# A two-layer recurrent block: the second attention's division moved to DMA and GpSimd, and q, k kept in DRAM with 32 rows to a head

## The chip, the cores and the metric

The kernel runs on one core of one Trainium2 chip. The metric is the device time of one execution in microseconds (us): the median over several runs. Engines are named as in the profile: PE is TensorE (PEld its weight loads), DVE is VectorE, ACT is ScalarE, POOL is GpSimd, and SP is SyncE, which here only issues DMA transfers. Each engine works through its own instructions in a fixed order; an instruction that waits holds up all that stand behind it on that engine. That holds for SP too, so a transfer that waits for its source delays the transfers behind it.

## The reference

Two layers follow each other on x of 2 x 2048 tokens with 256 features. Each layer normalizes x, computes an attention s and a gate g = silu(ffn), and adds s * g to x. All is float32. The attention has 16 heads of 16 features; the first layer's sees all tokens, the second's only a band of 64 tokens to either side.

```python
def attention(x, w_qkv, b_qkv, w_out, b_out):        # second layer; the first has no mask
    q, k, v = split_heads(x @ w_qkv + b_qkv)         # (b, 16 heads, 2048, 16)
    scores = einsum('bhqd,bhkd->bhqk', q, k) * SCALE + mask
    attn = softmax(scores, axis=-1)
    out = einsum('bhqk,bhkd->bhqd', attn, v)
    return merge_heads(out) @ w_out + b_out
x = L0_attn_x
for attn, ffn in ((L0_attn, L0_ffn), (L1_attn, L1_ffn)):
    xn = layernorm(x)
    x = x + attn(xn) * silu(ffn(xn))
```

The first layer's ffn is a mixture of eight low-rank experts with a cumulative sum over tokens, the second's a base product with eight small experts. The change does not touch their arithmetic.

## The kernel before

x, the normalized xn and the gates gt lie in SBUF with the features in the partitions: 128 partitions, two halves of features (NC = 2), 2048 tokens, one tile for each of the two batches b. The stages follow each other: layer norm and products of weights, the first ffn (`hidden`, `weights`, the loop over `ch` with `we`, `px`, `py`, `po`), `attention(A0, ..., False, False)`, the second layer norm with its ffn, and `attention(A1, ..., True, True)`. In the last call `local` is true: the band.

`attention` works on items (b, g, n): batch, group g of four heads (NG = 4), block n of 512 tokens (TB); 32 items a layer, n innermost. Q and K are projected by `keys_queries`, given their bias by ACT and stored to the DRAM tile qd; `fetch` brings a group's q and k back, so that each of the four heads has 32 partitions (HP = 32) of which 16 (HD) hold features. Four small matmuls then run side by side on PE. In k the 17th row of a head is 1, and in q it holds minus the row's maximum, so that the product gives scores less the maximum. The other rows of q are zero: a zero row set comes from the DRAM tile zd. Two q and two k tiles take turns, so a group is fetched while the one before it is worked on; in the second layer in two halves of 1024 tokens.

An item takes U steps: 16 in the first layer, 2 in the second. A step of `scores` issues PE's products sq (queries in the partitions, for the maxima) of an item some steps ahead, and sk (keys in the partitions) of the current one. DVE reduces sq to maxima (L611, in the second layer L606 with the mask), ACT takes the exponentials of sk (L615), and in the second layer POOL clears what lies outside the band (`affine_select`, L620). `place_max` (L631 on) turns an item's maxima by a PE transpose pmx, DVE negates them (row, L638), and four DMAs put them into q. This stands LEAD = 3 steps before the item's first sk. `weigh` multiplies the exponentials with v, DEL steps later (acc, L662). v has a column of ones per head, so acc holds in rows HD of each head's 32 the sum by which the head must be divided; ACT (and in the first layer POOL, L673) gathers acc in av. In PSUM, the tag "m" of pool `pm` has four banks, shared by sk, acc, pmx, tr, of and pr; pool `pmax` has two for sq.

The division differs in the two layers. In the first, `compact` sends the sums of av to DRAM (rd) and the 16 data rows of each head straight to xn; `invert` fetches the sums as 128 x 16 (dn) and takes the reciprocal on DVE; `spread` writes them to DRAM and fetches them broadcast to 16 rows per head (recb); `divide` multiplies on POOL (L753). In the second, `normalize` transposes av by four PE transposes (tr, L687), DVE takes reciprocals (L689) and multiplies (L690), and when the four groups of a block are done, `features` transposes back (of, L703) and ACT copies (L705). `project` then multiplies with the output weights (pr, L761), DVE with the gate (upd, L766), POOL adds to x (L767), and in the last layer the block is sent out (L769).

When a part runs is given in steps: the loop calls `at(step, f, ...)`, and after each step's products the parts due are issued. The build then orders the instructions of each engine by these and by what they depend on; `tc.keep_in_program_order` holds an instruction at the place where it was written.

```python
at(i * U - LEAD, place_max, i)
end = (i + 1) * U
if local:
    at(end + DEL, normalize, i)
```

Of the kernel before, what the change touches and what calls it, by code (L numbers as in the profile page):

```python
# [10 lines left out]
F32 = mybir.dt.float32  # L11
# [6 lines left out]
P = 128  # L18
D = 256
# [18 lines left out]
def two_layers(ctx: ExitStack, tc: tile.TileContext, a, out):  # L38
# [113 lines left out]


    with tc.tile_pool(name="fw", bufs=1) as fw:
        FV = fw.tile([P, NC, 2 * KE * R0], F32, name="FV")
# [246 lines left out]
    def attention(A, scale, local, final):  # L402
# [14 lines left out]
        with ExitStack() as st:  # L417
            pool = lambda name, bufs, **kw: st.enter_context(tc.tile_pool(name=name, bufs=bufs, **kw))
            kq, vp, dr = pool("kq", 1), pool("vp", 1), pool("dr", 1, space=bass.MemoryType.DRAM)
            qd = dr.tile([2, B, D, T], F32, name="qd")  # L420
            vs = [vp.tile([P, NV, (H - 1) * HV + HP], F32, name=f"v{b}", tag=f"v{b}") for b in range(B)]
            qs = [kq.tile([P, T], F32, name=f"q{i}", tag=f"q{i}") for i in range(2)]
            ks = [kq.tile([P, T + 2 * PAD], F32, name=f"k{i}", tag=f"k{i}") for i in range(2)]
            zd = dr.tile([NG, T], F32, name="zd")

            rd = [[dr.tile([NG, TB], F32, name=f"rd{i}{k}", tag=f"rd{i}{k}") for k in range(2)] for i in range(2)]
            for t in qs:
                nc.gpsimd.memset(t, 0.0)
# [80 lines left out]
            def fetch(bg, lo=0, hi=T):  # L509

                if bg >= B * NG:
                    return
                b, g = divmod(bg, NG)
                k0, k1 = max(lo - PAD, 0), (T if hi == T else hi - PAD)
                for i, t in ((1, qs[bg % 2]), (0, ks[bg % 2])):
                    to, s = (slice(lo, hi), slice(lo, hi)) if i else (slice(PAD + k0, PAD + k1), slice(k0, k1))
                    for j in range(NG):
                        h = g * NG + j
                        nc.sync.dma_start(out=t[j * HP : j * HP + HD, to], in_=qd[i, b, h * HD : (h + 1) * HD, s])

                nc.sync.dma_start(out=qs[bg % 2][HD:P:HP, lo:hi], in_=zd[:, lo:hi])

# [107 lines left out]
            def place_max(i):  # L630
# [43 lines left out]

            def heads(b, n):

                return xn[0 if local else b].rearrange("p c t -> p (c t)")[:, bass.ts(n, TT * D)].rearrange(
                    "p (t h w) -> p t h w", h=H, w=HD
                )

            def normalize(i):

                b, g, n = items[i]
                av = avs.pop(i)
                ps = pm.tile([P, TT, NG, HP], F32, name="tr", tag="m")
                for t in range(TT):
                    nc.tensor.transpose(ps[:, t].rearrange("p j w -> p (j w)"), av[:, bass.ts(t, P)], ident)  # L687
                rec = op.tile([P, TT, NG], F32, name="rec", tag="rec", bufs=2)
                nc.vector.reciprocal(rec, ps[:, :, :, HD])  # L689
                nc.vector.tensor_tensor(  # L690
                    heads(b, n)[:, :, g * NG : (g + 1) * NG, :], ps[:, :, :, :HD],
                    rec[:, :, :, None].to_broadcast([P, TT, NG, HD]), ALU.mult,
                )

            feats = {}

            def features(i, c):

                b, g, n = items[i]
                ot = heads(b, n).rearrange("p t h w -> p t (h w)")  # L700
                ps = pm.tile([P, TB], F32, name="of", tag="m")
                for t in range(TT):
                    nc.tensor.transpose(ps[:, bass.ts(t, P)], ot[:, t, bass.ts(c, P)], ident)  # L703
                f = op.tile([P, TB], F32, name="f", tag=f"f{c}", bufs=2 if local else 1)
                nc.scalar.copy(f, ps)  # L705
                feats[b, n, c] = f

            def together(b, g, n):


                lo = g % 2 * NG * HD
                return xn[b][lo : lo + NG * HD, g // 2, bass.ts(n, TB)]

            divs = {}

            def compact(i):

                b, g, n = items[i]
                av = avs.pop(i)
                nc.sync.dma_start(out=rd[i % 2][0], in_=av[HD:P:HP, :])  # L720
                for j in range(NG):
                    nc.sync.dma_start(out=together(b, g, n)[j * HD : (j + 1) * HD, :], in_=av[j * HP : j * HP + HD, :])

            def flat(d):
                return d.rearrange("j (r e) -> (j r) e", r=P // NG)

            def invert(i, step):

                if step == 0:
                    divs[i] = op.tile([P, NG * TB // P], F32, name="dn", tag="dn", bufs=2)  # L730
                    tc.keep_in_program_order(nc.sync.dma_start(out=divs[i], in_=flat(rd[i % 2][0])))
                else:
                    tc.keep_in_program_order(nc.vector.reciprocal(divs[i], divs[i]))

            def spread(i, step):

                b, g, n = items[i]
                if step == 0:
                    tc.keep_in_program_order(nc.sync.dma_start(out=flat(rd[i % 2][1]), in_=divs[i]))
                    return  # L740
                recb = op.tile([P, TB], F32, name="recb", tag="recb", bufs=2)
                lo = g % 2 * NG * HD
                for j in range(NG):
                    tc.keep_in_program_order(nc.sync.dma_start(
                        out=recb[lo + j * HD : lo + (j + 1) * HD, :], in_=rd[i % 2][1][j, :].partition_broadcast(HD)
                    ))
                divs[i] = recb[lo : lo + NG * HD, :]

            def divide(i):

                b, g, n = items[i]
                tc.keep_in_program_order(
                    nc.gpsimd.tensor_tensor(together(b, g, n), together(b, g, n), divs.pop(i), ALU.mult)  # L753
                )

            def project(i, oc):
# [3 lines left out]
                for c in range(NC):  # L760
                    nc.tensor.matmul(  # L761
                        pr, A["o"][:, c, bass.ts(oc, P)], feats[b, n, c] if local else xn[b][:, c, cols],
                        start=(c == 0), stop=(c == NC - 1),
                    )
# [16 lines left out]
            for i, (b, g, n) in enumerate(items):  # L781
                at(i * U - LEAD, place_max, i)
                end = (i + 1) * U
                if local:
                    at(end + DEL, normalize, i)
                    if g == NG - 1:
                        for c in range(NC):
                            at(end + DEL + 1 + c, features, i, c)
                        for oc in range(NC):
                            at(end + DEL + 3 + oc, project, i, oc)  # L790
                else:

                    for r, (f, *step) in enumerate(
                        ((compact,), (invert, 0), (invert, 1), (spread, 0), (spread, 1), (divide,))
                    ):
                        at(end + DEL + (0, 2, 4, 5, 7, 11)[r], f, i, *step)
                    if g == NG - 1:
                        for oc in range(NC):
                            at(end + DEL + 13 + oc, project, i, oc)
                if local and n == NB // 2 - 1:  # L800
# [218 lines left out]
```

## Time and profile before

| what | value |
|---|---|
| median of 3 runs | 2620.93 us (2620.79 to 2621.52) |
| profiled execution, its own time | 2619.84 us |
| its span, first to last instruction | 2618.1 us |
| mean granted TensorE clock | 0.991 |
| PE busy | 2570.3 us (98% of the span) |
| DVE, ACT, POOL busy | 1671.5, 1641.1, 894.9 us |
| first layer's attention in the span | about 475 to 2142 us |
| second layer's attention | about 2246 to 2618 us |

The profile shows one execution. Busy times are shares of an engine's own span; since matmuls are pipelined and their ends are modelled, a busy PE is read for where it stands idle rather than as a measure of its rate. A group of instructions is given with its source line, engine, tile names, shape, count, busy time, mean duration, and the idle time before it with what ended it. The timeline gives starts and durations; a bracket holds the idle time before an instruction and what ended it. SPq is the issuing of transfers on SP.

### The profile page before, as it was taken

To read this page: it belongs to the slowest core of one execution; us is meant where nothing else is said; L and a number is where in the kernel's file an instruction comes from. 1 tells how busy PE (TensorE), PEld (TensorE's weight loads), DVE (VectorE), ACT (ScalarE), POOL (GpSimd) and SP (SyncE) were. 2 spreads that over 40 slices of the span, in tenths; PEclk is the share of its full clock that TensorE was granted. 3 is DMA by queue.
4 is the path that set the end of the run, shared out by engine and by line. 5 is a ranking of instruction groups with operands and counts; after the bars stand their busy time and mean duration, and the time that the engine had idled before them with its cause. 6 is when DMAs were issued, how large, how long until landed. Compare 5 with 4: busy or idle time off the path is not lost.

```text
span 2618.1 us, 49275 instructions
## 1 busy us (share of the span) xinstructions
PE 2570.3 (98%) x19060; PEld 1099.6 (42%) x19060; DVE 1671.5 (64%) x2753; ACT 1641.1 (63%) x3200; POOL 894.9 (34%) x845
## 2 busy tenths in 40 slices
PE   8999999999999999999999999999999978999999
PEld 5444444543333333333333333333333324558776
DVE  4133332167888888888777888888888523228884
ACT  5300000228888888888778888888888854236655
POOL 0000000203444444444444444444444430206666
PEclk9999999999999999999999999999999989989999
DMA  4031110410001010010010010010000012411120
GB/s 150 3 88 45 53 45 32 99 64 4 8 12 19 8 24 9 6 25 8 6 25 8 6 25 8 6 27 6 8 8 6 10 30 35 96 67 39 46 58 35
DMA packets 58857, 82.08 MB, mean 31 GB/s; under 512 B 24160, under 2 KB 29152, under 8 KB 57040
## 3 DMA queue, kind: packets, MB, share of 16 engines
q1 hardware_dynamic: 56576, 77.36, 12.3%
q8 instruction: 150, 2.46, 0.4%
q10 hardware_dynamic: 2048, 1.58, 0.2%
q14 instruction: 83, 0.68, 0.1%
HBM read 52.22 MB, written 21.95 MB: 28 GB/s over the span
## 4 chain that ended last, share of the span: by engine, by line
PE 97%; DVE 1%; ACT 1%; DMA 0%; issue 0%; POOL 0%; SPq 0%; POOLq 0%; ACTq 0%; DVEq 0%
PE sk L599 25%; PE acc L662 22%; PE sq L599 19%; PE pp L446 4%; PE py L377 4%; PE po L357 4%; PE px L373 4%; PE ph L263 2%; PE pr L761 2%; PE pp L459 2%; PE psf L199 1%; PE po L909 1%; PE tr L687 1%; PE xb L127 1%; PE po L389 1%; PE xt L104 1%
## 5 line engine op out<-in xcount | busy, mean ns | idle before, releaser
L611 DVE TENSOR_REDUCE part<-sq 128x2 f32<-128x1024 f32 x1024 | 1206.7, 1220 | 304.2 <-PE sq L599 303.7
L615 ACT ACTIVATE e<-sk 128x512 f32<-128x512 f32 x2048 | 1062.7, 615 | 214.9 <-PE sq L599 192.2
L599 PE MATMUL sk<-q,k 32*128 32x512 f32 (+2 forms) x5632 | 1149.7, 533 | 0.6 <-ACT e L615 0.4
L599 PE MATMUL sq<-k,q 32*128 32x512 f32 (+2 forms) x5120 | 1140.8, 572 | 3.2 <-DVE part L611 1.7
L673 POOL TENSOR_TENSOR av<-av,more 128x512 f32<-128x512 f32 x480 | 607.7, 1266 | 961.2 <-ACT more L672 961.1
L599 PEld LDWEIGHTS sk<-q,k 32*128 32x128 f32 x5632 | 532.3, 184 | 581.1 <-ACT e L615 490.9
L662 PE MATMUL acc<-e,v 128*32 128x512 f32 x4096 | 550.6, 605 | 0.0
L599 PEld LDWEIGHTS sq<-k,q 32*128 32x128 f32 x5120 | 412.5, 184 | 28.0 <-DVE part L611 14.0
L672 ACT COPY more<-acc 128x512 f32<-128x512 f32 x480 | 287.8, 600 | 3.8 <-PE acc L662 1.7
L662 PEld LDWEIGHTS acc<-e,v 128*32 128x32 f32 x4096 | 82.4, 108 | 391.5 <-ACT e L615 387.0
L393 ACT ACTIVATE gt<-po 128x512 f32<-128x512 f32 x16 | 9.5, 596 | 324.6 <-PE po L389 324.6
L606 DVE CUSTOM_DVE_ANT_0 seen<-sq,mask 128x256 f32<-128x256 f32 (+1 forms) x512 | 177.4, 411 | 41.5 <-PE sq L599 32.8
L399 POOL TENSOR_TENSOR x<-x,up 128x512 f32<-128x512 f32 x16 | 20.2, 1264 | 416.4 <-DVE up L396 416.4
L620 POOL TENSOR_SCALAR_AFFINE_SELECT xn<-xn 128x512 f32<-128x512 f32 x172 | 103.1, 635 | 119.3 <-ACT xn L615 117.4
L381 DVE TENSOR_TENSOR xs<-we,px 128x512 f32<-128x512 f32 x64 | 43.8, 685 | 135.4 <-PE px L373 135.4
L373 PE MATMUL px<-xn,FV 128*128 128x512 f32 x256 | 121.2, 595 | 0.0
L377 PE MATMUL py<-cum,FW 128*128 128x512 f32 x256 | 120.5, 593 | 0.6 <-DVE cum L346 0.6
L615 ACT ACTIVATE xn<-sk 128x512 f32<-128x512 f32 x172 | 90.1, 601 | 48.2 <-PE sk L599 12.9
L357 PE MATMUL po<-pr,UO 128*128 128x512 f32 x256 | 119.0, 592 | 0.0
L383 DVE TENSOR_TENSOR pr<-xs,py 128x512 f32<-128x512 f32 x64 | 44.0, 687 | 62.4 <-PE py L377 62.2
L766 DVE TENSOR_TENSOR upd<-gt,pr 128x512 f32<-128x512 f32 x32 | 22.0, 687 | 86.0 <-PE pr L761 79.5
L357 PEld LDWEIGHTS po<-pr,UO 128*128 128x128 f32 x256 | 48.6, 190 | 61.2 <-issue 60.7
(169 smaller groups left out, 1683.2 us busy)
## 6 DMA issues: line engine op xcount, KB each, us to landing
we<-wd SPq DMA_DIRECT2D x128, 128.0 KB
qd<-sb SPq DMA_DIRECT2D x48, 256.0 KB
k<-qd SPq DMA_DIRECT2D x40, 128.0 KB
q<-qd SPq DMA_DIRECT2D x40, 128.0 KB
x<-in_x SPq DMA_DIRECT2D x8, 512.0 KB
q<-row SPq DMA_DIRECT2D x256, 2.0 KB
xn<-av SPq DMA_DIRECT2D x128, 32.0 KB
recb<-rd SPq DMA_DIRECT2D x128, 32.0 KB
```

Of the source, the lines that this page charges most:

```text
L357: nc.tensor.matmul(po[oc], UO[:, ch, bass.ts(oc, P)], pr, start=(ch == 0), stop=False)
L373: nc.tensor.matmul(px, FV[:, c, bass.ts(ch, P)], xn[b][:, c, cols], start=(c == 0), stop=(c == NC - 1))
L377: nc.tensor.matmul(py, FW[:, c, bass.ts(ch, P)], cum[:, c, :], start=(c == 0), stop=(c == NC - 1))
L446: nc.tensor.matmul(ps, w[:, c, bass.ts(hf, P)], xn[b][:, c, bass.ts(n, TB)], start=(c == 0), stop=(c == NC - 1))
L599: nc.tensor.matmul(o, lhs, rhs, start=True, stop=True)
L606: nc.vector.tensor_tensor_reduce(seen[:, lo:hi], sq[:, d, t * 2 * P + lo : t * 2 * P + hi], mask[:, lo:hi], 1.0, LOWEST, ALU.add, ALU.max, ...
L611: nc.vector.tensor_reduce(pt[:, pair[0] : pair[1] + 1, t, kb], sq, AX.X, ALU.max)
L615: nc.scalar.activation(e, t, AF.Exp, scale=scale)
L620: nc.gpsimd.affine_select(out=e[:, :, c, :], in_=e[:, :, c, :], compare_op=ALU.is_ge, fill=0.0, base=0, pattern=[[0, 4], [sign, P]], chann ...
L662: nc.tensor.matmul(acc[hp[j], o : o + hi - lo], vs[b][:, kt, vcols(g, j)], es[j][:, lo:hi], start=(r == 0), stop=(r == len(parts) - 1), sk ...
L672: nc.scalar.copy(more, acc)
L673: nc.gpsimd.tensor_tensor(avs[i], avs[i], more, ALU.add)
```

## The change

qd becomes one DRAM tile for both layers with 32 rows to a head, of which the 16 rows that are not features are filled once, early in the first ffn's stage: with ones for k, zeros for q. A group's q or k is then one transfer of 128 rows, and zd and the settings of q and k by POOL are left out. `place_max` writes an item's maxima by one transfer.

The division goes the same way in both layers: `away` sends av whole to DRAM (ad), `compact` fetches the sums (dn) and the data rows (to xn) in one transfer each, `invert` takes the reciprocal on DVE and writes it to DRAM, `spread` fetches it broadcast in one transfer, and `divide` multiplies on POOL. These steps stand 0, 1, 2, 3 and 5 steps after an item's last `weigh` in the second layer, and the projection 6 after it. `normalize` and `features` are gone.

```diff
+    qd = ctx.enter_context(tc.tile_pool(name="qd", bufs=1, space=bass.MemoryType.DRAM)).tile(
+        [2, B, H, HP, T], F32, name="qd"
+    )
...
+        zeros = fw.tile([P, TB], F32, name="zeros")
+        nc.vector.memset(zeros, 0.0)
+        for b in range(B):
+            for i, t in ((0, ones), (1, zeros)):
+                for half in range(NC):
+                    nc.sync.dma_start(
+                        out=qd[i, b, bass.ts(half, H // NC), HD:, :], in_=t[:, None, :].to_broadcast([P, NB, TB])
+                    )
...
-            qd = dr.tile([2, B, D, T], F32, name="qd")
-            zd = dr.tile([NG, T], F32, name="zd")
-            rd = [[dr.tile([NG, TB], F32, name=f"rd{i}{k}", tag=f"rd{i}{k}") for k in range(2)] for i in range(2)]
-            for t in qs:
-                nc.gpsimd.memset(t, 0.0)
-            for t in vs + ks:
+            ad = [dr.tile([NG, HP, TB], F32, name=f"ad{i}", tag=f"ad{i}") for i in range(3)]
+            rd = [dr.tile([NG, TB], F32, name=f"rd{i}", tag=f"rd{i}") for i in range(3)]
+            for t in vs:
                 nc.gpsimd.memset(t, 1.0)
-            nc.sync.dma_start(out=zd, in_=qs[0][:NG, :])
...
-                nc.sync.dma_start(out=qd[i, b, bass.ts(hf, P), bass.ts(n, TB)], in_=sb)
+                nc.sync.dma_start(out=qd[i, b, bass.ts(hf, H // NC), :HD, bass.ts(n, TB)], in_=sb)
...
-                    for j in range(NG):
-                        h = g * NG + j
-                        nc.sync.dma_start(out=t[j * HP : j * HP + HD, to], in_=qd[i, b, h * HD : (h + 1) * HD, s])
-                nc.sync.dma_start(out=qs[bg % 2][HD:P:HP, lo:hi], in_=zd[:, lo:hi])
+                    nc.sync.dma_start(out=t[:, to], in_=qd[i, b, bass.ts(g, NG), :, s].rearrange("h w t -> (h w) t"))
...
-                for j in range(NG):
-                    nc.sync.dma_start(
-                        out=q[j * HP + HD : j * HP + HD + 1, bass.ts(n, TB)].rearrange("o (t c) -> o t c", c=P),
-                        in_=row[j * TT : (j + 1) * TT, :],
-                    )
+                nc.sync.dma_start(out=q[HD:P:HP, bass.ts(n, TB)].rearrange("j (t c) -> j t c", c=P), in_=row)
...
-                    avs[i] = op.tile([P, TB], F32, name="av", tag="av", bufs=2)
+                    avs[i] = op.tile([P, TB], F32, name="av", tag="av", bufs=3 if local else 2)
...
+            pin = tc.keep_in_program_order
+            def away(i):
+                pin(nc.sync.dma_start(out=ad[i % 3].rearrange("j w f -> (j w) f"), in_=avs.pop(i)))
...
+            def compact(i):
+                divs[i] = op.tile([P, NG * TB // P], F32, name="dn", tag="dn", bufs=3)
+                pin(nc.sync.dma_start(out=divs[i], in_=ad[i % 3][:, HD, :].rearrange("j (r e) -> j r e", r=P // NG)))
+                pin(nc.sync.dma_start(out=together(*items[i]), in_=ad[i % 3][:, :HD, :]))
+            def invert(i):
+                pin(nc.vector.reciprocal(divs[i], divs[i]))
+                pin(nc.sync.dma_start(out=flat(rd[i % 3]), in_=divs[i]))
+            def spread(i):
+                lo = items[i][1] % 2 * NG * HD
+                recb = op.tile([P, TB], F32, name="recb", tag="recb", bufs=2)
+                divs[i] = recb[lo : lo + NG * HD, :]
+                pin(nc.sync.dma_start(out=divs[i], in_=rd[i % 3][:, None, :].to_broadcast([NG, HD, TB])))
...
-                        pr, A["o"][:, c, bass.ts(oc, P)], feats[b, n, c] if local else xn[b][:, c, cols],
+                        pr, A["o"][:, c, bass.ts(oc, P)], xn[0 if local else b][:, c, cols],
...
+                hops = (0, 1, 2, 3, 5, 6) if local else (0, 2, 4, 7, 11, 13)
+                for hop, f in zip(hops, (away, compact, invert, spread, divide)):
+                    at(end + DEL + hop, f, i)
+                if g == NG - 1:
+                    for oc in range(NC):
+                        at(end + DEL + hops[-1] + oc, project, i, oc)
```

More of the change, by code (lines that the diff above doesn't have):

```diff
@@ L673, in weigh @@
                     nc.gpsimd.tensor_tensor(avs[i], avs[i], more, ALU.add)
[L675 to L706, printed above, removed]
@@ L708, in together @@
             def together(b, g, n):
                 lo = g % 2 * NG * HD
-                return xn[b][lo : lo + NG * HD, g // 2, bass.ts(n, TB)]
+                return xn[0 if local else b][lo : lo + NG * HD, g // 2, bass.ts(n, TB)]
             divs = {}
[L716 to L722, printed above, removed]
+            pin = tc.keep_in_program_order
@@ L724, in flat @@
+            def away(i):
+                pin(nc.sync.dma_start(out=ad[i % 3].rearrange("j w f -> (j w) f"), in_=avs.pop(i)))
             def flat(d):
                 return d.rearrange("j (r e) -> (j r) e", r=P // NG)
[L727 to L740, printed above, removed]
-                recb = op.tile([P, TB], F32, name="recb", tag="recb", bufs=2)
[L742 to L746, printed above, removed]
+            def compact(i):
+                divs[i] = op.tile([P, NG * TB // P], F32, name="dn", tag="dn", bufs=3)
+                pin(nc.sync.dma_start(out=divs[i], in_=ad[i % 3][:, HD, :].rearrange("j (r e) -> j r e", r=P // NG)))
+                pin(nc.sync.dma_start(out=together(*items[i]), in_=ad[i % 3][:, :HD, :]))
@@ L751, in divide @@
                 b, g, n = items[i]
-                tc.keep_in_program_order(
+                pin(
                     nc.gpsimd.tensor_tensor(together(b, g, n), together(b, g, n), divs.pop(i), ALU.mult)
@@ L783, in attention @@
                 end = (i + 1) * U
[L784 to L799, printed above, removed]
+                hops = (0, 1, 2, 3, 5, 6) if local else (0, 2, 4, 7, 11, 13)
[4 more added lines that the diff above has]
+                        at(end + DEL + hops[-1] + oc, project, i, oc)
                 if local and n == NB // 2 - 1:
```

## The prediction

> **What bounds the kernel now.** I read the page first, for the chain that ended last: it is TensorE almost throughout.
>
> ```profile
> PE 97%; DVE 1%; ACT 1%; DMA 0%; issue 0%; POOL 0%; SPq 0%; POOLq 0%; ACTq 0%; DVEq 0%
> ```
>
> So an edit is worth what it takes off PE's queue, and costs whatever makes PE wait. The stretches are next (length, busy time and count by engine, clock, DMA share, GB/s): the second layer's attention, and the end of the span.
>
> ```profile
> 2400.00:2500.00 100.00, 99.48 (x1641) 77.01 (x1635) 80.46 (x424) 61.36 (x128) 64.47 (x102) 1.00 0.18 52
> 2590.00:2618.00 28.00, 22.11 (x159) 12.02 (x158) 7.09 (x13) 7.00 (x14) 13.71 (x15) 0.97 0.20 75
> ```
>
> PE is full in the loop, but DVE (80%) and POOL (64%) are not far off. The groups by shape give what goes (tr, of) and what POOL does and will do more of:
>
> ```profile
> L687 PE MATMUL tr<-ident,av 128*128 128x128 f32 x128 | 20.5, 283 | 0.0
> L703 PE MATMUL of<-ident,xn 128*128 128x128 f32 x64 | 9.8, 276 | 0.0
> L620 POOL TENSOR_SCALAR_AFFINE_SELECT xn<-xn 128x512 f32<-128x512 f32 x172 | 103.1, 635 | 119.3 <-ACT xn L615 117.4 <-PE acc L662 1.1 <-PE sq L599 0.8
> L753 POOL TENSOR_TENSOR xn<-xn,recb 64x512 f32<-64x512 f32 x32 | 40.6, 1269 | 11.2 <-DMA recb<-rd 10.0
> ```
>
> Their means overlap in the pipeline, so the timeline of one item (two steps) gives the price:
>
> ```profile
> 2560.30 0.35 PEld L599 LDWEIGHTS sk<-q,k 32*128 32x128 f32 x3
> ...
> 2563.02 2.40 POOL L620 TENSOR_SCALAR_AFFINE_SELECT xn<-xn 128x512 f32<-128x512 f32 x4 [1.23 <-ACT xn L615]
> ...
> 2563.55 0.42 PEld L687 LDWEIGHTS tr<-ident,av 128*128 128x128 f32 x4 [0.20 <-ACT xn L615]
> ...
> 2564.14 0.19 PEld L599 LDWEIGHTS sk<-q,k 32*128 32x128 f32 x2 [0.17 <-ACT av L667]
> ...
> 2567.58 0.35 PEld L599 LDWEIGHTS sk<-q,k 32*128 32x128 f32 x3
> ```
>
> The step with the four transposes takes 3.84 us (2560.30 to 2564.14), the next, with a pmx in their place, 3.44: an item is 7.28. The first layer already divides by DMA, and its last item shows the chain bare:
>
> ```profile
> 2125.23 0.53 SPq L720 DMA_DIRECT2D rd<-av  x1
> ...
> 2128.32 0.53 SPq L731 DMA_DIRECT2D dn<-rd  x1
> 2130.04 0.25 DVE L733 RECIPROCAL dn<-dn 128x16 f32<-128x16 f32 x1 [7.56 <-DMA dn<-rd]
> 2130.32 0.34 SPq L739 DMA_DIRECT2D rd<-dn  x1
> 2131.76 1.71 SPq L744 DMA_DIRECT2D recb<-rd  x4
> 2135.18 1.26 POOL L753 TENSOR_TENSOR xn<-xn,recb 64x512 f32<-64x512 f32 x1 [9.98 <-DMA recb<-rd]
> ```
>
> A read of sums lands 1.72 us after its issue, a write of inverses 1.44, the spread 3.42.
>
> **The change part by part.**
>
> 1. Transposes gone. For the 28 items whose normalize stands before the last steps: the four transposes fill 0.43 us of PE (0.107 apart), and PE then waits 0.17 for av's copy because tr holds one of four PSUM banks. Between 0.43 and 0.60 an item; I take 0.55, near the upper end, since the bank is freed too: 28 x 0.55 = 15.4. For batch 0's last group `features` goes as well: 8 x 0.43 = 3.4. Together -18.8. On DVE the 0.25 + 0.42 us of L689 and L690 become one 0.24 reciprocal (L733's row); ACT loses sixteen 0.60 us copies. Both lie beside PE and count nothing.
>
> 2. POOL. Each item adds one 1.27 us multiply to eight selects of 0.60 (four in 2.40 above): 6.1 us of an item that PE would do in 6.7. It fits, barely. The multiply stands between the selects in POOL's order; a step's selects are then done some 6.4 us into the step and PE's acc reads them at about 8.9 (two steps later), so 1.27 more is covered by 2.5 us. Were that cover gone, an item would cost POOL's time.
>
> 3. The DMA hops, per item: away (256 KB), dn, xn, rd, recb, where there was none. In SP's order, per item: row, rd(i), away(i+1), recb(i), dn(i+1), xn(i+1). The reciprocal is fixed in DVE's order and the multiply in POOL's. Behind a late reciprocal stand the next eight maxima of DVE, then PE, with two sq buffers only. The loop: after recip(i), rd issues (0.4 us), then away(i+1), landing 2.1 (1.44 for a write, plus 256 KB at the rate below, 0.7), dn 2.0, reciprocal 0.25: 4.8 us, against 6.7 an item. 1.9 us are spare. recb lands some 4 us before POOL's multiply. [...]
>
> ```profile
> 2270.00:2271.00 1.00, 1.00 (x4) 0.48 (x3) 0.00 (x0) 0.41 (x1) 0.00 (x0) 1.00 0.61 229
> 2284.00:2285.00 1.00, 1.00 (x6) 0.87 (x6) 0.56 (x2) 0.00 (x0) 0.00 (x0) 1.00 1.01 123
> ```
>
> The first row (2 KB stores of q, k) is 229 / 0.61 = 375 GB/s, 23 an engine. On 4 engines recb's 128 KB take 1.4 us, so it lands in 2.9; on 16 it would be 1.8. [...]
>
> 4. Fetches. A group's q, k go from 1 MB in 16-row pieces (plus zeros) to 2 MB in 128-row transfers. The second row above is the old form at full load: 123 GB/s. [...] At 123 GB/s a half fetch of both would hold the rings 8 us; at 375, 2.8. I take 2.8, less than the 4 us of the old one. Both fetches stand in front of hops of the loop: twelve such half fetches, each within the spare 1.9 to 2.1. For these and for rows of maxima that land near their use: +1.5 (0 to 8; below 0 nothing, PE did not wait there).
>
> 5. One transfer for maxima where there were four (0.6 us of SP instead of 2.5), no zd, no memsets of q, k: SP and POOL time with nothing late behind it. 0 (-2 to +2). Eight 1 MB fills of DRAM are new: they come behind the last small load, at 31 us, on SP, and the next DMA of SP is at 115; on 8 engines 8 x 5.6 = 45 us, hidden. If not hidden they would delay the first wd store, thus PE.
>
> 6. First layer's end. Chain from the last av: away 2.1 + dn 2.0 + 0.28 + 1.47 + recb 2.9 = 8.9, where 2125.20 to 2135.18 was 10.0: -1.1 (-2.5 to +1). Its other 31 divisions have 16 steps an item: covered.
>
> 7. The kernel's end. Before, PE is past the last item quickly:
>
> ```profile
> 2578.54 1.16 PE L599 MATMUL sk<-q,k 32*128 32x256 f32 x24
> ...
> 2608.38 3.73 PE L761 MATMUL pr<-f,wo 128*128 128x512 f32 x8
> ...
> 2612.99 1.26 POOL L767 TENSOR_TENSOR x<-x,upd 128x512 f32<-128x512 f32 x1 [0.45 <-DVE upd L766]
> ```
>
> From 2578.54 (the first step without maxima) to the end: 39.6 us. After, all sixteen pr matmuls (eight projections) of the last group come behind the last acc, and POOL's order is select, divide, two adds, divide, two adds: four blocks in series. POOL's selects and three divides end at 2.5 + 20 x 0.6 + 3 x 1.3 = 18.4. A block: divide 1.27, two projections, upd, add 5.9 (2608.38 to 2614.25), handing over 0.1: 7.3. Then 3.9 from the last add to the end. 18.4 + 29.2 + 3.9 = 51.5: +11.9 (9 to 15). The last item's hops (done about 39 us in; its divide is due at 40.3) hide behind these blocks.
>
> Sum: -18.8 + 1.5 + 0 - 1.1 + 11.9 = -6.5. The profiled execution took 2619.84 (span 2618.1 and 1.74 around it), so 2613.3; the median is 1.09 above it: 2614.4.
>
> **The rivals.** (A) The forecast: the loop gains, two thirds go back at the end. Own range 2608 to 2622.
> (B) Slower: the hop loop of part 3 becomes the period. For it: a small write at 789.54 in the first layer, behind a fetch, had its follower issued only at 793.84, 4.3 us; no row shows 256 KB out and back, nor 4-engine transfers. Against: 1.9 us spare. It decides once the hops exceed 6.7 us; at 7.4 it is 0.7 x 28 = 20 us: 2634.
> (C) POOL becomes the bound (the transposes leave, but not their time): with 0.1 us lost at each of nine POOL instructions an item takes 7.0, not 6.7; 0.3 x 28 = 8: 2623.
> (D) The end overlaps better, 6 instead of 11.9, and an item gains 0.60: 2607.
> That the transposes do not leave is excluded: in the order of instructions PE has none of them.
>
> **How the numbers follow.** A 0.55, B 0.22, C 0.13, D 0.10. 0.2% (5.2 us, about what can be told from no change) puts the line at 2615.7. A gives 0.34 faster, 0.18 same, 0.03 slower; B slower; C 0.08 same, 0.05 slower; D faster: 0.44, 0.26, 0.30. The range, 2606 to 2638, leaves out half of D and the upper part of B.
>
> **What would show it.** Right: item period near 6.7 us between rows of maxima, POOL near 90% in the loop, DVE waiting for dn under 2 us in the loop's total, the last affine select to the last add near 29 us. Wrong: POOL waiting for recb or DVE for dn in most items (B); POOL at 99% with PE waiting for selects (C); a 128-row fetch at 123 GB/s; fills still running at 115 us; any PE wait in the first layer.

## The result, and the profile after

The changed kernel takes 2628.55 us (median of 11 runs, 2624.76 to 2634.20) where the kernel before took 2620.79 beside it: a ratio of 1.0034 (95% interval 1.0025 to 1.0044). It is slower by about 8 us. The forecast was 2614.4, faster; the time lies in the range, the sign is wrong. The profiled execution has a span of 2626.0 us, against 2618.1.

The page first: its busy row, the chain that ended last with its lines, and the row of the scores' matmuls (busy, mean ns, then idle time before them and what ended it).

```profile
PE 2541.2 (97%) x18868; PEld 1074.7 (41%) x18868; DVE 1657.9 (63%) x2722; ACT 1630.1 (62%) x3184; POOL 921.8 (35%) x869
PE 91%; DMA 4%; DVE 2%; POOL 1%; ACT 1%; issue 1%; SPq 0%; POOLq 0%; ACTq 0%; DVEq 0%
...
L605 PE MATMUL sk<-q,k 32*128 32x512 f32 (+2 forms) x5632 | 1150.6, 536 | 23.9 <-DMA q<-row 21.3
```

TensorE lost 192 matmuls, the transposes, and is busy 29.1 us less. Yet the span is longer: 4% of the chain are transfers, and for the first time TensorE stands idle for one, the row of maxima. The two stretches shown of the kernel before (the second one moved with the end; length, busy time and count of PE, PEld, DVE, ACT, POOL, then clock, DMA share, GB/s):

```profile
2400.00:2500.00 100.00, 88.07 (x1507) 65.30 (x1505) 71.42 (x396) 53.98 (x116) 76.24 (x110) 0.95 0.45 139
2590.00:2626.00 36.00, 19.48 (x62) 7.63 (x58) 6.12 (x11) 0.74 (x2) 18.15 (x17) 0.86 0.29 102
```

In the loop TensorE is busy 88 of 100 us where it was 99.5, and its granted clock is 0.95 where it was 1.00; the DMA share went from 0.18 to 0.45. The waits (us in total, times, longest) name what is late:

```profile
DVE dn L700 <- DMA dn<-ad: 52.4, 20, 9.0
...
PE sk L605 <- DMA q<-row: 21.3, 11, 3.6
...
PE pr L722 <- POOL xn L714: 20.7, 4, 12.6
```

To see where 8 us come from, I cut the span at VectorE's `row<-pmx` instructions of the second layer, one for each of 32 items (counted from 0):

| stretch | before, us | after, us | difference | forecast |
|---|---|---|---|---|
| start to row 1 | 2350.6 | 2336.5 | -14.0 | -1.1 |
| row 1 to row 31 (the loop) | 230.4 | 240.9 | +10.6 | -17.3 |
| row 31 to the end | 37.2 | 48.5 | +11.4 | +11.9 |

The end came as forecast. The other two are each wrong by more than the result: a gain that was not in the sum, and a loop that lost 28 us more than it was given. They hide each other in the total, so that the time lies in the stated range is luck.

The loop itself, in the chain of waits (start, us, what), behind the fetches that were issued at 2363.36 and 2364.46:

```profile
2366.19 5.27 DMA rd<-dn
2371.46 0.02 issue
2371.47 0.54 SPq L708
...
2372.67 0.51 SPq L697
...
2373.27 4.20 DMA q<-row
2377.47 0.14 issue
2377.60 0.76 PE sk L605
```

SyncE issues the write of inverses (rd), then stands at the spread (L708) for 5.27 us until that write has landed behind 1 MB of q and k. VectorE made the row of maxima from 2368.98 to 2369.25; it is issued only at 2373.27, after the spread, the read of sums (L696) and that of the heads' data rows (L697), and lands 4.20 us later. TensorE had nothing to do for 2.23 us. What comes next is seen in the clock column (the last but two):

```profile
2374.00:2376.00 2.00, 1.29 (x26) 0.81 (x25) 0.95 (x6) 1.68 (x4) 1.44 (x3) 1.00 0.27 66
2376.00:2377.00 1.00, 0.00 (x0) 0.00 (x0) 1.00 (x7) 0.00 (x0) 1.00 (x2) 1.00 0.56 186
2377.00:2381.00 4.00, 3.40 (x44) 3.12 (x48) 2.20 (x14) 1.08 (x2) 1.18 (x3) 0.57 0.27 82
```

From 2377.0 us the clock is halved for 3.4 us. From 2340 to 2580 us the clock's mean is 0.95, so 12 us of full speed are missing; the kernel before has 1.00 from 2350 to 2581.

### The profile page after: what moved, and what is told of

The parts are those of the page before. It is cut to its first block, busy times and chain, and to the rows that moved or that the text cites. A ratio compares the mean times of both kernels' runs of the same rounds, so it can differ in the third digit from the quotient of the medians.

```text
span 2626.0 us, 48011 instructions
## 1 busy us (share of the span) xinstructions
PE 2541.2 (97%) x18868; PEld 1074.7 (41%) x18868; DVE 1657.9 (63%) x2722; ACT 1630.1 (62%) x3184; POOL 921.8 (35%) x869
## 4 chain that ended last, share of the span: by engine, by line
PE 91%; DMA 4%; DVE 2%; POOL 1%; ACT 1%; issue 1%; SPq 0%; POOLq 0%; ACTq 0%; DVEq 0%
PE sk L605 23%; PE acc L664 21%; PE sq L605 18%; PE py L391 4%; PE po L371 4%; PE pp L456 4%; PE px L387 4%; PE ph L277 2%; PE pr L722 2%; DMA q<-row 2%; PE pp L469 2%; PE psf L204 1%; PE po L861 1%; PE xb L127 1%; PE pt L855 1%
## 5 line engine op out<-in xcount | busy, mean ns | idle before, releaser
L605 PE MATMUL sk<-q,k 32*128 32x512 f32 (+2 forms) x5632 | 1150.6, 536 | 23.9 <-DMA q<-row 21.3
L714 POOL TENSOR_TENSOR xn<-xn,recb 64x512 f32<-64x512 f32 x64 | 81.5, 1273 | 14.7 <-DMA recb<-rd 12.3
L722 PE MATMUL pr<-xn,wo 128*128 128x512 f32 x128 | 66.1, 646 | 20.7 <-POOL xn L714 20.7
```

The lines of the kernel that those rows point to most:

```text
L605: nc.tensor.matmul(o, lhs, rhs, start=True, stop=True)
L722: nc.tensor.matmul(pr, A["o"][:, c, bass.ts(oc, P)], xn[0 if local else b][:, c, cols], start=(c == 0), stop=(c == NC - 1),)
```

## The experiments

Theory S: the loop's loss is twelve half fetches standing in front of hops and rows of maxima. Rivals: the loop of hops is too long by itself (H), or POOL is at its limit (P). The ratio is to the kernel before as it ran beside each kernel (medians of 2619.7 to 2620.8 us). The two stretches come from the one profiled execution of each, which can lie up to 6 us from the median (f1_turn: 2600.88).

| kernel | median us | ratio to before (95%) | row 1 to 31, us | row 31 to end, us |
|---|---|---|---|---|
| before | 2620.79 | 1 | 230.4 | 37.2 |
| after | 2628.55 | 1.0034 (1.0025 to 1.0044) | 240.9 | 48.5 |
| e1_nofetch | 2602.46 | 0.9931 (0.9918 to 0.9945) | 213.1 | 51.1 |
| e2_order | 2614.19 | 0.9977 (0.9969 to 0.9985) | 221.3 | 57.4 |
| e3_quarters | 2633.41 | 1.0050 (1.0038 to 1.0063) | 242.4 | 50.1 |
| e5_actq | 2631.43 | 1.0042 (1.0029 to 1.0054) | 240.9 | 50.0 |
| e6_late | 2644.11 | 1.0088 (1.0074 to 1.0101) | 248.2 | 55.2 |
| e7_end | 2629.46 | 1.0036 (1.0022 to 1.0049) | 240.0 | 47.0 |
| e8_olddiv | 2606.80 | 0.9947 (0.9935 to 0.9960) | 229.9 | 36.9 |
| e9_all | 2636.01 | 1.0055 (1.0041 to 1.0069) | 247.6 | 48.8 |
| f1_turn | 2595.05 | 0.9904 (0.9889 to 0.9920) | 222.9 | 37.1 |
| f2_quart | 2596.90 | 0.9911 (0.9898 to 0.9923) | 221.0 | 36.8 |
| g1_ramp | 2607.63 | 0.9955 (0.9942 to 0.9968) | 230.2 | 37.2 |
| h1_pieces | 2724.21 | 1.0398 (1.0384 to 1.0412) | 333.7 | 50.3 |
| h2_pieces16 | 2621.62 | 1.0007 (0.9998 to 1.0016) | 233.3 | 49.2 |
| h3_halfcols | 2610.44 | 0.9962 (0.9950 to 0.9975) | 222.9 | 49.0 |

**No fetches in the loop.**

```diff
-                if local and n == NB // 2 - 1:
-                    at(end, fetch, b * NG + g + 2, 0, T // 2)
-                if n == NB - 1:
+                if not local and n == NB - 1:
```

> Leaves out the twelve half fetches of q and k in the second layer's loop (groups from the third on are computed from stale q and k; all other work is kept). Theory S (transfers of 1 MB stand in front of hops and rows of maxima; twelve stalls of about 2.9 us, half of it the 3.4 us of half clock that follows an idle TensorE): the items take 6.5 us throughout, no dip of the clock in the loop, 253 us from first to last row of maxima become about 222, so 2628.6 - 31 = about 2597. Rival H (the loop of hops, reciprocal to reciprocal, is itself too long): items stay irregular, 2620 or more. Rival P (POOL at its limit): items of 7 us, 2615.

Measured: 2602.46 us, 5 us over the number of theory S, and the loop in 213.1. Four items take 6.81, 6.53, 6.53 and 6.05 us where the kernel before had 7.39, 7.27, 7.25 and 6.77: 0.7 us an item gained. Theory S holds; H and P, which asked for irregular items or items of 7 us, fall. The fetches cost 240.9 - 213.1 = 28 us in this loop. The same six issues of SyncE without a fetch near them:

```profile
2392.20 0.32 SPq L701 DMA_DIRECT2D rd<-dn  x1
2392.61 0.38 SPq L688 DMA_DIRECT2D ad<-av  x1
2393.66 0.54 SPq L708 DMA_DIRECT2D recb<-rd  x1
2394.69 0.51 SPq L696 DMA_DIRECT2D dn<-ad  x1
2395.26 0.51 SPq L697 DMA_DIRECT2D xn<-ad  x1
2395.89 0.56 SPq L645 DMA_DIRECT2D q<-row  x1
```

The spread goes out 1.46 us after rd, not 5.28. The end keeps its 51 us, so it is a matter of its own.

**Another order on SyncE.** The row of maxima first, `away` ahead of the write of inverses, the read of sums ahead of the spread, by registering the steps in that order (both layers):

```diff
+            todo = ((away, hops[0]), (compact, hops[1]), (invert, hops[2]), (spread, hops[3]), (divide, hops[4]))
+            for i in range(len(items)):
+                at(i * U - LEAD, place_max, i)
+            for f, hop in todo:
+                for i in range(len(items)):
+                    at((i + 1) * U + DEL + hop, f, i)
             for i, (b, g, n) in enumerate(items):
-                at(i * U - LEAD, place_max, i)
                 end = (i + 1) * U
...
-                for hop, f in zip(hops, (away, compact, invert, spread, divide)):
-                    at(end + DEL + hop, f, i)
```

> Only SyncE's order changes: in each step the row of maxima first, the write of av ahead of the write of inverses, the read of sums and heads ahead of the spread; the fetches stay where they are, with the same bytes. If SyncE standing at the spread until the inverses have landed is what makes rows and sums late: most of the stalls go, 2628.6 - 20 = about 2609. If the rings being full of the fetch is what does it (rows and sums behind 1 MB, whoever issued first): at most a third goes, 2620 or more. Rival P: no change, 2628.

Measured: 2614.19 us, between the two numbers and nearer the first: 14.4 us won, 19.6 in the loop. Every row of maxima is now issued within 0.04 us of being made (up to 4.6 us in the kernel after), the wait of TensorE for q<-row is gone, and the clock is 1.00 throughout the loop. So SyncE's standing wait was the larger part of the stall. What stays is waits of VectorE for sums and of POOL for the spread. The end grew to 57.4 us; its chain is POOL's series of products and additions, and what made it longer than in the kernel after was not tried alone.

**Quarters.**

```diff
-                if local and n == NB // 2 - 1:
-                    at(end, fetch, b * NG + g + 2, 0, T // 2)
-                if n == NB - 1:
-                    at(end, fetch, b * NG + g + 2, T // 2 if local else 0)
+                if local:
+                    at(end, fetch, b * NG + g + 2, n * TB, (n + 1) * TB)
+                elif n == NB - 1:
+                    at(end, fetch, b * NG + g + 2)
```

> The same bytes of q and k are fetched in quarters, after every item of a group instead of after every second: 512 KB at a time. Theory S with a spare of 1.9 us in the loop of hops: 1.4 us of transfer stay under it, most stalls go: about 2604 (2598 to 2615). If the sum of bytes counts (bandwidth), or the number of issues on SyncE: 2628 or more.

Measured: 2633.41 us; the miss is plain. The spare of 1.9 us hides none of these transfers: rd to spread takes 2.9 to 5.1 us in 16 of the 24 items up to the last fetches, TensorE waits 22.0 us for rows (21.3 in the kernel after), and the loop has 242.4 us. The second theory's number holds.

**The fetch from ScalarE.**

```diff
-                    at(end, fetch, b * NG + g + 2, 0, T // 2)
+                    at(end, fetch, b * NG + g + 2, 0, T // 2, nc.scalar)
```

(and so for the second half)

> The half fetches in the second layer's loop are issued by ScalarE instead of SyncE: same bytes, same moments, another ring. If hops and rows suffer by standing behind the fetch in one ring: they pass it, stalls mostly gone, about 2605. If the 16 engines are shared and all slow down alike: a half or less goes, 2615 to 2625. If ScalarE is held up by waiting for free q and k: slower than 2628.

Measured: 2631.43 us, not to be told from the kernel after; the first theory's number is missed by 26. The third names a time like this one, but ScalarE is not held up: its longest wait in the loop is 4.1 us, against 5.4 in the kernel after. From rd to the spread it is now mostly 1.5 to 3 us, but the sums wait in its place: dn to reciprocal takes up to 7.4 us (up to 5.2 in the kernel after), and TensorE still idles 19.4 us for rows. Here another queue only moved the wait.

**Fetches behind the spread**, on top of the changed order: `at(end + 1, fetch, ...)` in place of `at(end, fetch, ...)`, pinned there.

> On top of the changed order of SyncE: the half fetches are issued after the spread of their step, so that a row of maxima and a read of sums never stand behind one; only the next write of av does. Order alone left 233.6 us from first to last row of maxima, no fetch at all 225.5. If the rest of the stalls is sums standing behind the fetch: about 228 us, 2614.2 - 5 = 2609 (2606 to 2611). If the write of av behind the fetch passes the delay on: no gain, 2613 to 2616.

Measured: 2644.11 us, worse than either number. Its SyncE shows why:

```profile
2393.84 0.46 SPq L527 DMA_DIRECT2D q<-qd  x1
2394.34 0.43 SPq L527 DMA_DIRECT2D k<-qd  x1
2394.82 0.46 SPq L688 DMA_DIRECT2D ad<-av  x1
2395.32 0.43 SPq L701 DMA_DIRECT2D rd<-dn  x1
```

The fetch now goes out right ahead of the write of av, whose landing the next read of sums waits for, and the reciprocal behind that; from rd to the spread it is 7.4 to 9.1 us in these items. It is the second rival of the text on record, and with a larger price. In the kernel with the changed order the fetch stood behind both writes, the one place in the cycle that nothing near follows but the row.

**The end on VectorE.**

```diff
+            def last(b, g):
+                return nc.vector if final and b == B - 1 and g == NG - 1 else nc.gpsimd
...
-                    nc.gpsimd.tensor_tensor(together(b, g, n), together(b, g, n), divs.pop(i), ALU.mult)
+                    last(b, g).tensor_tensor(together(b, g, n), together(b, g, n), divs.pop(i), ALU.mult)
```

(and so for the addition to x)

> The kernel after with one edit: the last group's four divisions and eight additions of the last sequence run on VectorE instead of POOL. If the end's 48.5 us (37.2 before the change) are POOL's series of divide, two products, two additions, four times: each block loses some 1.5 us, 42 to 44 us, 2628.6 - 5 = about 2623. If the last item's hops set the end, under 1 us is won: 2628.

Measured: 2629.46 us, no gain; its end takes 47.0 us instead of 48.5. The rival holds: once POOL's series is shorter, the last items' hops set the end (its chain there is transfers, up to the last recb<-rd).

**All three together.**

> SyncE's changed order, the fetches after the spread, and the end's divisions and additions on VectorE, all together. If the three act on different stretches they add up: 2609 - 6 to 10 = about 2600 (2597 to 2605), under both kernels. If the end is set by hops that the earlier loop only makes wait: 2606 to 2610.

Measured: 2636.01 us. It inherits the late fetch (247.6 us in the loop); against that variant the end won 6.4 us (48.8 for 55.2). So the series matters where it is not hidden by the hops, and hops and series both have to go.

**The division of before, all else after.** `normalize` and `features` come back for the second layer, `away` to `divide` stay in the first.

> The kernel after, but the second layer's heads are divided as in the kernel before (transposes, features); q and k with 32 rows to a head, whole-group fetches and maxima in one transfer stay. If division by hops is what suffers from the fetches: without hops the rows stand at most behind 1 MB, which their 5 us of slack cover; item 7.28 us, end 37 us, about 2612 (2604 to 2616). If the fetches hurt by themselves: 2620 or more.

Measured: 2606.80 us, within the first range: all that is new but the division is worth 14 us, and the division by hops costs 2628.55 - 2606.80 = 21.8. The loop is that of the kernel before (229.9 against 230.4) and so is the end; the whole gain lies ahead of row 1.

**TensorE's order at the second layer's start.** In the kernel before, only the matmuls of that stretch are pinned to the order of the program:

```diff
-                    nc.tensor.matmul(o, lhs, rhs, start=True, stop=True)
+                    mm = nc.tensor.matmul(o, lhs, rhs, start=True, stop=True)
+                    if local and not second:
+                        tc.keep_in_program_order(mm)
```

(and so for the second sequence's projections and values)

> The kernel before, with one thing changed: TensorE's order where the second layer begins (the first item's scores for maxima between the second sequence's projections) is pinned to the order of the program, which is the order that the kernel after has there; in the kernel before 64 of these matmuls stand in one row, 13.5 us long, paced by VectorE and at half clock. If that order is what brought the kernel after to its first items 14 us earlier: 2620.3 - 10 = about 2610 (2608 to 2613). If it is the faster fetch or the memsets gone: 2618 or more.

Measured: 2607.63 us, 12 us under the kernel before without touching a transfer. The chain of the kernel before, and of this one, over the same work:

```profile
2302.28 3.63 PE pp L446 x8
2305.91 1.09 PE sq L599 x16
...
2308.54 10.74 PE sq L599 x48
```

```profile
2296.39 0.97 PE sq L603 x16
2297.36 10.50 PE pp L446 x24
2307.86 1.08 PE sq L603 x16
2308.93 10.50 PE pp L446 x24
2319.43 1.08 PE sq L603 x16
```

Before, 48 matmuls for maxima stand in a row and go at VectorE's pace, 10.74 us for what takes 3 x 1.08 where projections stand between them. The clock column of the kernel before, and of this one, over 42 us of that stretch:

```profile
2299.00:2341.00 42.00, 40.44 (x151) 21.82 (x151) 11.57 (x66) 10.02 (x18) 0.00 (x0) 0.84 0.20 76
```

```profile
2296.00:2338.00 42.00, 42.00 (x198) 24.65 (x197) 14.23 (x81) 14.89 (x29) 0.00 (x0) 1.00 0.23 88
```

0.16 x 42 = 6.7 us of full speed are missing there. The kernel after has the better order as a by-product: its q and k are in place in fewer, larger transfers, and the scheduler that orders the instructions placed the scores between the projections. That this is why the scheduler did so is argued only; that the order is worth 12 us is measured. In the profile of the kernel after, this stretch holds 10.4 of the 14.0 us ahead of row 1: its first projection of keys starts 3.6 us earlier than before (2242.64 against 2246.20). Where these 3.6 us come from was not tried.

**The last group by transposes again**, with SyncE's changed order: the four items of the last group take `normalize`, a transpose back of their 64 columns and a copy, all other items the hops.

```diff
+                if bare(i):
+                    at(end + DEL, normalize, i)
+                    at(end + DEL + 1, features, i)
                 if g == NG - 1:
                     for oc in range(NC):
-                        at(end + DEL + hops[-1] + oc, project, i, oc)
+                        at(end + DEL + (2 if bare(i) else hops[-1]) + oc, project, i, oc)
```

> SyncE's changed order (fetches where they were), and the last group of the last sequence is divided by transposes on TensorE and VectorE again; all other items keep the hops. Order alone: 2614.2, with 57.4 us behind the last row of maxima, where the kernel before and the one with transposes throughout have 37. If the end's excess is the hops and the POOL series of the last group: about 39 us, less four items at 0.75 lost: 2614 - 15 = about 2599 (2596 to 2603), under the 2606.8 of transposes throughout. If the end waits for something earlier (hops of the third group, POOL's selects): 2606 to 2612.

Measured: 2595.05 us, 1 us under the first range; 1% under the kernel before and 12 us under the kernel with transposes throughout (e8_olddiv). Its end is 37.1 us, with TensorE at work almost to the last addition:

```profile
2584.87 1.80 PE pr L755 x4
2586.67 0.44 PE tr L699 x4
2587.11 1.72 PE pr L755 x4
2588.83 0.44 PE of L713 x4
2589.26 1.81 PE pr L755 x4
```

So the hops and the series of the last group were the end's excess. This is the version that beats both kernels.

> As the kernel with changed order and a transposed last group, and fetches in quarters, 512 KB after each item. In the kernel after, quarters made it 5 us slower, since they put a fetch in front of every row and every read of sums. With rows and sums no longer behind SyncE's wait, a quarter's 1.4 us stay under the 2.5 us that a read of sums has: loop 233.6 to about 228 us, 4 us under the variant with halves. If any fetch between the write of av and the read of sums costs its own time: equal or up to 4 us slower than the variant with halves.

Measured, with quarters on top: 2596.90 us, loop 221.0 against 222.9. The intervals overlap, so no difference between halves and quarters is shown once rows and sums are ahead on SyncE; neither number of the expectation can be told from the other. The loop without fetches (213.1) is not reached; what holds these last 8 us was not tried.

**What it is in a fetch that costs.** One half fetch in eight pieces:

```diff
+                    if local and bg >= 2:
+                        for j in range(NG):
+                            nc.sync.dma_start(
+                                out=t[j * HP : j * HP + HD + i, to], in_=qd[i, b, g * NG + j, : HD + i, s]
+                            )
+                    else:
...
```

> The kernel after, but in the second layer's loop q and k come in pieces of 17 and 16 rows, a head each: half the bytes, eight transfers for two. If the bytes of the fetch are what delays hops and rows: 2628.6 - 12 = about 2616. If it is the time that the rings are held (16-row pieces ran at 123 GB/s in the kernel before, so 4.3 us for a half fetch against 2.8) and SyncE's 0.4 us for each of eight issues: 2634 or more.

Measured: 2724.21 us, far over the rival's number. For microseconds on end its transfers move no more than this (the last two columns, DMA share and GB/s):

```profile
2404.00:2408.00 4.00, 4.00 (x76) 3.31 (x76) 2.93 (x16) 2.55 (x6) 2.22 (x4) 0.82 0.06 23
```

A share of 0.06 is what one busy engine of the 16 would give (1/16), and it moves 23 GB/s; the whole fetch of the kernel after moved 382 GB/s at a share of 1.02 (2367 to 2368 us). Each q piece has 17 rows. At a rate so much lower the run says nothing on bytes. The next two do.

```diff
+                    if local and bg >= 2:
+                        for j in range(NG):
+                            nc.sync.dma_start(out=t[j * HP : j * HP + HD, to], in_=qd[i, b, g * NG + j, :HD, s])
+                        if i:
+                            nc.sync.dma_start(out=t[HD:P:HP, to], in_=qd[i, b, bass.ts(g, NG), HD, s])
...
```

> The kernel after, but in the second layer's loop q and k come in pieces of 16 rows, a head each, and a strided transfer of zeros, as in the kernel before: half the bytes, nine transfers for two. If the 17-row pieces were slow because each ran on one engine: far under their 2724. If the held rings and SyncE's issues count (16-row pieces at 123 GB/s hold a half fetch 4.3 us, nine issues take 3.8 us of SyncE): 2635 to 2660, over the 2628.6 of one transfer with twice the bytes. If bytes count: about 2616.

Measured: 2621.62 us. Sixteen rows, not 17: 103 us less. And 7 us under the kernel after: half the bytes in nine transfers are better than all in two, so the single transfer of 32 rows to a head is no gain inside this loop. The expectation that held engines and issues outweigh the bytes is refuted; the time is 6 us over the number for bytes alone.

```diff
+                    if local and bg >= 2:
+                        to, s = slice(to.start, (to.start + to.stop) // 2), slice(s.start, (s.start + s.stop) // 2)
```

> The kernel after, but each half fetch in the second layer's loop brings only the first half of its columns, in the same transfers at the same moments (the rest of q and k stays stale, all other work is kept): 0.5 MB instead of 1. No fetch at all gave 2602.5, the full one 2628.6. If a stall is the transfer's time less the spare: 1.4 us instead of 2.8, most of it under the spare, 2605 to 2612. If any fetch in front of a hop costs, whatever its size: 2618 to 2628.

Measured: 2610.44 us, in the first range. Over the loop without fetches (213.1), twelve fetches of 0.5 MB cost 9.8 us, twelve of 1 MB 27.8, and 24 of 0.5 MB (the quarters) 29.3. So the bytes count, and more than in proportion: half of them cost a third. Why was not tried. The form counts too: the run before moves the same bytes as this one in nine transfers instead of two and takes 11 us longer; TensorE waits 22.9 us for rows there and 10.1 here. Which of the issues, the rows to a transfer or the length of its runs does it stays open.

## Why the prediction was wrong

1. *Transposes gone, -18.8.* Right in kind and nearly in size. An item away from fetches gains 0.7 us where 0.55 was given (6.5 us an item, not 6.7), but the whole loop without fetches gains 230.4 - 213.1 = 17.3. Part of the rest lies where the first sequence ends, a place the sum does not have: from 2440 to 2500 us of that run VectorE waits 8.8 us for sums, and behind that TensorE 1.8 us for maxima, with 3.4 us at half clock after it. The chain of waits leads there from POOL's addition to the sending out of a finished block (out<-x, issued at 2489.11), the spread behind it on SyncE (2489.60) and a read of sums that takes 4.03 us. It is the stall of point 4 with another large transfer (512 KB) in the fetch's place.
2. *POOL, 0.* Right: POOL is busy 87 of 100 us in the loop without fetches, and items of 6.5 us stand beside that. Rival C falls.
3. *The hop loop, 4.8 us with 1.9 spare.* Right without a fetch: reciprocal at 2391.93 and the next sums issued at 2394.69 (e1_nofetch), and 2.0 to 2.2 us from that issue to the reciprocal where VectorE waits for it (e6_late): 4.8 to 5.0 together. No run shows the 2.9 of the sum for the spread, nor the four engines behind it and behind the 2.0 for a read of sums: in the bare chain of point 6 the spread took 3.72 and the read 2.09. There the spread moves 59 to 68 GB/s at a DMA share of 0.17 to 0.20, slower than the 94 GB/s that 1.4 us for 128 KB asked for. Nothing waited long for it in the loop of the kernel after.
4. *Fetches, +1.5 (0 to 8).* This is the step that failed. The rate was right (2367 to 2368 us: 382 GB/s at a share of 1.02). But "each within the spare 1.9 to 2.1" took the transfer's time as the whole delay and looked at one path, dn to reciprocal. In the order of SyncE that the prediction itself gives, the row stands behind the spread's wait for rd. A fetch ahead of rd thus held the row twice: on SyncE, up to 4.6 us, and on the DMA engines, 4.2 us in the stall shown, where it waited 4.0 on SyncE. The row had some 6 us to spare (made at 2369.25, TensorE out of work at 2375.37). And five of the seven waits for rows over 1.8 us drew 3.4 us or more at half clock after them, some 10 us of full speed, a term the sum does not have. In place of 1.5 the fetches cost 28 us, of which another order on SyncE alone takes 19.6 away (e2_order).
5. *Maxima in one transfer, no zd, fills, 0.* Right for the fills: they run from 31 to about 76 us, the 45 us forecast, at a DMA share of 0.52 and 204 GB/s (eight of 16 engines, the number in the forecast, would give 0.50), and no wait is put down to them. From 27 us on the kernel after is late by 1.7 us, but by a half clock (below). Missing here is a step that the sum does not have at all: the order of TensorE at the second layer's start, worth 12 us alone in the kernel before. It could be read from the order of instructions of both kernels ahead of any run, and the prediction asked that order only whether the transposes had gone.
6. *First layer's end, -1.1.* Wrong in sign, small:

```profile
2123.08 1.99 DMA ad<-av
...
2125.13 2.09 DMA dn<-ad
...
2127.52 2.25 DMA rd<-dn
2129.78 0.02 issue
2129.79 3.72 DMA recb<-rd
```

From the last av to the end of the product it is 11.9 us (2123.06 to 2134.99), against 11.3 before (2125.22 to 2136.49): the write of inverses takes 2.25 where 1.44 was taken, the spread 3.72 where 2.9 was. (The forecast's terms for this chain add to 8.75, not 8.9; that changes nothing.)

7. *The kernel's end, +11.9 (9 to 15).* Right in size: +11.4. The mechanism is half right: the last blocks go in series on POOL, but the last item's hops do not hide behind them:

```profile
2608.28 2.52 DMA rd<-dn
...
2610.81 3.73 DMA recb<-rd
...
2614.70 1.27 POOL xn L714
...
2616.02 2.09 PE pr L722 x2
```

The series of POOL and the hops end close together: shortening the series alone took 1.5 us off the end and nothing off the median, and the hops alone were not taken away. That the sum comes out so near is partly luck, since the hops were to be hidden.

Of the rivals, B named the right resource and sign ("the hop loop becomes the period"), with the small write behind a fetch in the first layer (4.3 us) as its evidence, and 2634 as its time. Its mechanism is only met in items with a fetch. That row was the nearest there was to this change, and it was the one to take for part 4: twelve fetches at 4.3 less 1.9 are 29 us. That this is almost what was measured is luck, for this sum has neither the row nor the clock in it.

## What to carry to other kernels

Price a transfer by what is queued behind it on its issuing engine and on the DMA engines, and by who waits for those: over the loop without fetches, the same 12 MB cost 8, 28 or 35 us here (e2_order, the kernel after, e6_late), depending on where in SyncE's order they stood. Put what the busiest engine waits for (here the row) ahead of every issue that waits itself, and never place a bulk transfer right ahead of a hop whose landing is the next step's condition. When a change alters transfers at a stage's start, compare the order of instructions on every engine over the whole kernel, not only where lines were removed.

## What the runs showed of the hardware

A short wait of TensorE cost twice in some places here. The same wait of 1.53 us ends at 20.17 us in the kernel after and at 20.18 in the kernel before (five us from 21 on, clock in the last but two columns; before, then after):

```profile
21.00:26.00 5.00, 5.00 (x37) 4.27 (x36) 3.13 (x12) 4.08 (x10) 0.00 (x0) 1.00 1.06 378
```

```profile
21.00:26.00 5.00, 5.00 (x23) 4.03 (x22) 2.56 (x7) 3.35 (x8) 0.00 (x0) 0.66 1.06 377
```

One execution lost 0.34 x 5 = 1.7 us to it, the other nothing. In e7_end and e8_olddiv, whose edits to the kernel after lie elsewhere, TensorE is idle for 1.67 us between 18 and 21 us, and the clock is 1.00 from 18 to 26. In the loop of the kernel after, waits of TensorE for rows of 0.72 to 0.94 us left the clock alone, and so did one of 1.90 and one of 2.17; waits of 1.84, 2.16, 2.23 and 3.60 us were each followed by 3.4 us at half, and one of 3.46 by 6.8. So the length of a wait alone did not tell, from 1.84 to 2.23 us, whether the clock fell; what does was not shown. A difference of 1.7 us at one place, as here, need not be an effect of an edit.

With q in pieces of 17 rows the transfers moved 23 GB/s at a DMA share of 0.06 for 4 us on end (h1_pieces, 2404 to 2408 us); with pieces of 16 rows, and the 17th rows in a transfer of their own, the kernel was 103 us faster (h2_pieces16, 2621.62 against 2724.21).
